# One form of step for a software-pipelined graph layer: transposes one group ahead, second layer in the present group, sums one group behind

## The chip, the cores and the metric

The kernel runs on one core of one Trainium2 chip. The metric is the device time of one execution in microseconds; the time before is the median of three runs. A profile was taken of a further execution of the same program, and all instants below are microseconds from the start of its span.

## What is computed

There are 12,500 nodes with 64 features and 200,000 edges, sorted by their destination. `ssp(v)` is softplus(v) minus ln 2.

```
gates    = (ssp(edge_attr @ We1 + be1) @ We2 + be2) * (1 - sigmoid(5 * (distance - 3.5)))
h        = ssp(concat(x[src], x[dst]) @ Wn1 + bn1) @ Wn2 + bn2
sums     = scatter_add(h * gates, at dst)
new      = x + ssp(sums @ Ws1 + bs1) @ Ws2 + bs2
out      = layernorm(x + new)
```

## The kernel before, in words

**Groups.** The edges are cut into NG = 391 groups of 512: four columns (K = 4) of 128 edges, one edge to a partition. Each step of the main loop (L581 to L655) works on several groups at once, each at another stage.

**The stages of a group g.**
- `gather(g)` (L190): up to four indirect DMAs on POOL bring the 64 source features of each edge into the tile `xg`. They are issued AHEAD = 14 groups ahead; a tile has 18 buffers. 24 of the columns are brought instead row by row by `fetch` (L206): four DMAs on the SP queue and four on the ACT queue in each of the first 384 steps, into `xr`.
- `load(g)` (L225): SP brings the edge features `eT` and, per half of a group, 42 rows of a table (`wns`) that holds the destination's share of the first layer. It is issued five groups ahead.
- `onehot(g)` (L240): DVE writes beside the gathered features a 42-wide one-hot of the destination.
- `transposes(g)` (L247): PE turns the four columns into a PSUM tile `tx`. `xcopy(g)` (L254): ACT copies it to SBUF.
- `layer1_edge(g)` and `layer1_node(g)` (L259, L265): PE writes 768 columns of the first layer to the PSUM tile `z`.
- `exps(g)` and `logs(g)` (L276, L281) on ACT, `softplus(g)` (L284) on DVE.
- `layer2_edge(g)` and `layer2_node(g)` (L290, L300) on PE into `gh`; `hcut(g)` and `message(g)` (L310, L314) on DVE.
- `scatter(g)` (L318): PE sums the messages by their one-hot; `window(g)` (L332): DVE adds the 42-wide result to `sums`.

PSUM tiles `z`, `gh` and `tx` have two buffers each.

**Node blocks.** When enough groups have been summed, a block of up to 512 nodes goes through its own small chain (`node_block`, L339): `hidden` and `layer2` on PE, activations on ACT, small work on DVE, and a store. Its parts are spread over later steps at the distances of BLOCK_STEPS. There are 25 blocks; the last is done after the loop.

**Order of the work.** The order on each engine is the order of the program text (`manual_schedule`); every engine's queue is in order. In the main form of the step (L588 to L618), step i issues on PE: the edge part of the second layer of group i-1, the first layer of group i+1, the sums of group i-3, the transposes of group i+3, and the node part of the second layer of group i-1. The first of these carries added waits for all that the step needs (`needs`, L589 to L592). On ACT the order is `exps(i+1)`, two row DMAs, `logs(i+1)`, two row DMAs, `xcopy(i+3)`. On DVE it is `hcut`, `message`, `window`, the node parts, `softplus(i+1)`, `onehot(i+5)`.

The last ten steps (L619 to L639, CATCH_UP = 10) have another form, in which the lags are taken back one at a time (`lagging`, L562 to L570): transposes, first layer, second layer, sums, in this order.

After the loop (L659 to L695) the last group and the last node block follow.

Of the kernel before, what the change touches and what calls it, by code (L numbers as in the profile page):

```python
# [56 lines left out]
P = 128  # L57
D = 64
HE = 256
GE = 2 * HE  # L60
W = 42
# [4 lines left out]
AHEAD = 14  # L66
LOADS = 5
SPREADS = 5
CATCH_UP = 10
PREPARE = 5  # L70
FREE = 5
BEHIND = 4
# [34 lines left out]
def gnn_resnorm_kernel(ctx: ExitStack, tc: tile.TileContext, a: dict, out: bass.AP, E: int):  # L107
# [18 lines left out]
    def z_tile():  # L126
        return psum.tile([P, 2, NB], F32, name="z")
# [4 lines left out]
    def tx_tile():  # L132
        return psum.tile([P, NB], F32, name="tx")
# [90 lines left out]

    def load(g):  # L225
        eTs[g] = loads.tile([P, HE], F32, name="eT")
        old = ("scatter", g - LOADS - 2 - 4)
        behind(note(("load", g), nc.sync.dma_start(eTs[g], a["eT"][:, g, :])), old)
        if g % 2 == 0:
            _, at = nc.values_load_multi_w_load_instructions(  # L230
                base_i[0:1, 2 * g : 2 * g + 4], engines=[SP], min_val=0, max_val=N - 1,
                skip_runtime_bounds_check_because="they were clamped to these bounds")
            bases[g], bases[g + 1] = at[:2], at[2:]
        for h in range(2):
            behind(note(("load", g), nc.sync.dma_start(wns[D:DW, g % REST, h, :], table[bass.ds(bases[g][h], W), :])),  # L235
                   old)
# [50 lines left out]
        nc.vector.scalar_tensor_tensor(ss[g].rearrange("p i t e -> p (i t e)")[:, part], us[g][:, part], BIG,  # L287
                                       z_of(g)[:, part], OP.min, OP.max)

    def layer2_edge(g, *needs):  # L290
        gh = gh_tile()
        v = gh.rearrange("p (i t h d) -> p i t h d", i=2, t=2, h=2)
        first = nc.tensor.matmul(gh, ones3[:, :P], row3.rearrange("q i k d -> q (i k d)"), start=True, stop=False,  # L293
                                 skip_group_check=True)
        behind(first, *needs)
        for t in range(2):
            nc.tensor.matmul(v[:, 0, t], ss[g][:, 0, t, :], we2, start=False, stop=False, skip_group_check=True)  # L297
        ghs[g] = gh.rearrange("p (i k d) -> p i k d", i=2, k=K)
# [7 lines left out]
    def layer2(g):  # L306
        layer2_edge(g)
        layer2_node(g)
# [118 lines left out]
    with tc.manual_schedule():  # L427
# [128 lines left out]
        with tc.tile_pool(name="finish", bufs=1) as finish:  # L556
            blocks = list(zip(node_blocks(N), block_steps(N, NG)))
            last = NG - 1
            ends = last - CATCH_UP
            second, third, ahead = {}, {}, {}  # L560

            def lagging(i, lag, steps):  # L562

                lag -= sum(i > step for step in steps)
                return [g for g in range(i - lag, i - lag + 1 + (i in steps)) if g >= 0]

            for i in range(-3, NG):
                second[i] = lagging(i, 1, (ends + 3,))
                third[i] = lagging(i, 3, (ends - 2, ends + 5))
                ahead[i] = [i + 3] if i < ends else [i + 2] if i == ends + 1 else [i + 1] if i > ends + 2 else []  # L570
            parts, begun, complete, rest = {}, None, 0, []

            def at(f, g, *more):
                if 0 <= g < NG:
                    f(g, *more)

            for g in range(LOADS - 3):
                load(g)
            for g in range(2):
                onehot(g)  # L580
            for i in range(-3, last - 1):  # L581
                now = parts.pop(i, [])
                early = [part for part in now if part.tensor]
                at(load, i + LOADS)
                fetch(i, nc.sync)
                if i >= 0:
                    at(gather, i + AHEAD, i < BEHIND)
                if i < ends:  # L588
                    needs = [("xcopy", i + 1), ("load", i + 1)]  # L589
                    needs += [(name, g) for g in ahead[i] for name in ("gather", "onehot")]  # L590
                    for g in second[i]:
                        layer2_edge(g, *needs)  # L592
                    if i >= -1:
                        zs[i + 1] = z_tile()
                        layer1_edge(i + 1)
                        for part in early:
                            part.tensor(tx_tile())
                    if i >= -1:
                        layer1_node(i + 1)
                    for n, g in enumerate(third[i]):  # L600
                        scatter(g, zs[i + 1][:, 1, HE + 2 * W * n : HE + 2 * W * (n + 1)])
                    at(exps, i + 1)
                    fetch(i, nc.scalar, 0, ROWS // 2)
                    at(logs, i + 1)
                    fetch(i, nc.scalar, ROWS // 2, ROWS // 2)
                    for g in ahead[i]:
                        transposes(g)
                        xcopy(g)
                    for g in second[i]:
                        layer2_node(g)  # L610
                    for g in second[i]:
                        hcut(g)
                        message(g)
                    for g in third[i]:
                        window(g)
                    for part in early:
                        part.others()
                    at(softplus, i + 1)  # L618
                else:  # L619
                    for g in ahead[i]:  # L620
                        transposes(g)
                        xcopy(g)
                    zs[i + 1] = z_tile()
                    layer1_edge(i + 1)
                    for part in early:
                        part.tensor(zs[i + 1][:, 1, HE:])
                    layer1_node(i + 1)
                    exps(i + 1)
                    logs(i + 1)
                    for g in second[i]:  # L630
                        layer2(g)
                        hcut(g)
                        message(g)
                    softplus(i + 1)
                    for g in third[i]:
                        scatter(g, tx_tile()[:, : 2 * W])
                        window(g)
                    for part in early:
                        part.others()  # L639
                for g in ahead[i]:  # L640
                    at(onehot, g + 2)
                for part in now:
                    if not part.tensor:
                        part.others()
                complete = third[i][-1] + 1 if third[i] else 0
                if blocks and complete >= blocks[0][1] - PREPARE and not begun:
                    begun = node_block(*blocks[0][0], finish)
                    begun.pop(0).others()
                if blocks and complete >= blocks[0][1]:
                    steps = next(steps for steps in BLOCK_STEPS if i + steps[-1] < last - 1)  # L650
                    for n, part in zip(steps, begun):
                        parts.setdefault(i + n, []).append(part)
                    rest = begun[len(steps) :]
                    blocks.pop(0)
                    begun = None  # L655
            assert len(blocks) == 1 and begun and not parts


            begun.pop(2).others()  # L659
            transposes(last)  # L660
            xcopy(last)
            zs[last] = z_tile()
            layer1_edge(last)
            layer1_node(last)
            for some in (edge, node):
                exps(last, some)
                logs(last, some)
            square, variance, root, scale, store = (part.others for part in rest)
            square()
            for g in range(last - 2, last + 1):  # L670
                window_bases(g)
            layer2(last - 1)
            scatter(last - 2, tx_tile()[:, : 2 * W])
            softplus(last, edge)
            hcut(last - 1)
            message(last - 1)
            layer2_edge(last)
            scatter(last - 1, tx_tile()[:, : 2 * W])
            softplus(last, node)
            window(last - 2)  # L680
            variance()
            root()
            layer2_node(last)
            window(last - 1)
            hcut(last)
            message(last)
            scatter(last, tx_tile()[:, : 2 * W])
            window(last)
            hidden, clamp = begun.pop(0)
            hidden(gh_tile())  # L690
            scale()
            clamp()
            store()
            for part in begun:
                node_part(part)  # L695
# [147 lines left out]
```

## Time and profile before

| | |
|---|---|
| median of three runs | 1989.88 us (1989.77 to 1997.46) |
| profiled execution | 1994.42 us, span 1992.6 us |
| granted TensorE clock, mean | 0.977 |
| PE busy | 1843.2 us, 92% of the span |
| DVE, ACT busy | 1082.5 us (54%), 925.0 us (46%) |
| POOL busy | 1463.8 us (73%), 1539 gathers |

A line of the timeline has the start, the duration, the engine, the line of the kernel, the operation, its tiles and shapes and its count; in brackets stands how long the engine was idle before it and what ended that. "issue" means that it waited for nothing that the profile shows. SPq and ACTq are DMA-issuing instructions of these engines. In the table by windows each engine has its busy time and, in brackets, its instructions; then come the granted share of the TensorE clock, the busy share of the DMA engines and the rate.

### The profile page before, as it was taken

What the parts mean: (1) busy time and instruction counts of PE and PEld (TensorE: products, weight loads), DVE (VectorE), ACT (ScalarE), POOL (GpSimd) and SP (SyncE); (2) the same over time, 40 slices, a digit from 0 to 9 for tenths busy, and PEclk for the clock granted to TensorE, in tenths of its full rate; (3) what the DMA queues carried; (4) which work ended last, traced back from release to release, by engine and by line L of the source; (5) the groups of instructions that cost most, each with busy time, mean ns of one, the idle gap of its engine ahead of it and who ended that gap; (6) DMA issues with size and microseconds to landing.
All of it is one profiled execution on the core that took longest, in us unless ns stands there. A gap on an engine that the chain in (4) does not pass through costs nothing.

```text
span 1992.6 us, 46151 instructions
## 1 busy us (share of the span) xinstructions
PE 1843.2 (92%) x11373; PEld 1531.6 (77%) x11373; DVE 1082.5 (54%) x2756; ACT 925.0 (46%) x1318; POOL 1463.8 (73%) x1543
## 2 busy tenths in 40 slices
PE   5899999999998998989999899999999999999996
PEld 4788788888777777777777777777887787787775
DVE  4455455555554554645555555555565555555554
ACT  1355455554444444544444444454454444455442
POOL 6777777777777777777777777777777777777770
PEclk9999899999999999999999999999899999999996
DMA  8422222222222222222232222232232222222230
GB/s 239 131 67 70 63 68 70 69 66 69 67 66 65 65 67 63 66 66 63 68 72 62 68 67 68 63 73 63 68 73 68 68 69 68 69 68 68 71 74 10
DMA packets 173687, 143.41 MB, mean 72 GB/s; under 512 B 49324, under 2 KB 145776, under 8 KB 173415
## 3 DMA queue, kind: packets, MB, share of 16 engines
q1 hardware_dynamic: 119758, 87.95, 15.3%
q0 software_dynamic: 49248, 50.53, 13.2%
q10 hardware_dynamic: 4408, 1.90, 0.4%
q8 instruction: 97, 1.59, 0.3%
q14 instruction: 176, 1.43, 0.2%
HBM read 130.57 MB, written 9.63 MB: 70 GB/s over the span
## 4 chain that ended last, share of the span: by engine, by line
PE 73%; SPq 8%; DMA 7%; issue 5%; DVE 2%; ACT 2%; ACTq 1%; POOL 1%; DVEq 0%; POOLq 0%
PE z L268 15%; PE gh L303 11%; PE gh L297 11%; PE z L262 10%; PE z L320 7%; PE tx L251 6%; PE gh L293 6%; DMA xr<-in_x 6%; PE z L260 3%; SPq L235 3%; SPq L219 2%; SPq L215 2%; PE z L530 2%; ACT u L279 2%; DVE h L312 1%
## 5 line engine op out<-in xcount | busy, mean ns | idle before, releaser
L202 POOL DMA_INDIRECT xg<-in_x,src_i x1539 | 1463.6, 951 | 477.8 <-issue 336.7
L279 ACT ACTIVATE u<-z 128x768 f32<-128x768 f32 x392 | 317.4, 810 | 659.1 <-PE z L320 625.3
L312 DVE TENSOR_TENSOR h<-gh,cut 128x256 f32<-128x256 f32 x391 | 166.1, 425 | 686.1 <-PE gh L303 669.8
L282 ACT ACTIVATE u<-u,one 128x768 f32<-128x768 f32 x392 | 365.9, 933 | 304.4 <-DMA xr<-in_x 294.6
L268 PE MATMUL z<-xT,wns 106*128 106x256 f32 x1564 | 415.9, 389 | 0.0
L303 PE MATMUL gh<-consts,s 128*128 128x64 f32 x3128 | 397.8, 271 | 0.0
L303 PEld LDWEIGHTS gh<-consts,s 128*128 128x128 f32 x3128 | 386.5, 194 | 0.0
L287 DVE SCALAR_TENSOR_TENSOR s<-u,z 128x768 f32<-128x768 f32 x392 | 372.8, 951 | 24.3 <-ACT u L282 7.2
L268 PEld LDWEIGHTS z<-xT,wns 106*128 106x128 f32 x1564 | 302.1, 195 | 44.8 <-ACT xT L256 0.7
L297 PE MATMUL gh<-consts,s 128*128 128x128 f32 x1564 | 280.8, 302 | 0.0
L262 PE MATMUL z<-eT,consts 128*128 128x256 f32 x782 | 277.7, 437 | 0.0
L297 PEld LDWEIGHTS gh<-consts,s 128*128 128x128 f32 x1564 | 205.8, 191 | 92.0 <-issue 91.4
L320 PEld LDWEIGHTS z<-xg,msg 128*128 128x128 f32 x1512 | 234.7, 196 | 21.6
L293 PE MATMUL gh<-row,ones 3*128 3x512 bf16 x391 | 148.9, 381 | 103.1 <-DMA xr<-in_x 47.8
L251 PE MATMUL tx<-consts,xg 128*106 128x128 f32 x1540 | 238.0, 278 | 4.0 <-DVE xg L241 2.7
L256 ACT COPY xT<-tx 106x512 f32<-106x512 f32 x391 | 222.4, 569 | 24.4 <-PE tx L251 15.3
L320 PE MATMUL z<-xg,msg 128*128 128x84 f32 x1512 | 221.6, 269 | 0.0
L337 DVE TENSOR_TENSOR sums<-sums,z 64x42 f32 x756 | 148.5, 196 | 129.9 <-issue 116.7
L251 PEld LDWEIGHTS tx<-consts,xg 128*106 128x106 f32 x1540 | 182.9, 144 | 5.2 <-DVE xg L241 3.0
L316 DVE TENSOR_TENSOR msg<-gh,h 128x256 f32<-128x256 f32 x391 | 165.9, 424 | 13.4
L262 PEld LDWEIGHTS z<-eT,consts 128*128 128x128 f32 x782 | 117.7, 190 | 47.6 <-issue 1.5
L293 PEld LDWEIGHTS <-ones 3*128 3x128 bf16 x391 | 35.5, 91 | 140.2 <-issue 122.1
(101 smaller groups left out, 685.5 us busy)
## 6 DMA issues: line engine op xcount, KB each, us to landing
eT<-in_eT SPq DMA_DIRECT2D x391, 128.0 KB
xg<-in_x,src_i POOLq DMA_INDIRECT x1539
xr<-in_x SPq DMA_DIRECT2D x1536, 0.2 KB
xr<-in_x ACTq DMA_DIRECT2D x1520, 0.2 KB
wns<-table SPq DMA_DIRECT2D x782, 21.0 KB
table<-tb SPq DMA_DIRECT2D x14, 448.0 KB
sums<-in_xT SPq DMA_DIRECT2D x7, 455.0 KB
y<-in_x SPq DMA_DIRECT2D x24, 128.0 KB
```

The costliest lines, as they stand in the source:

```text
L202: note(("gather", g), nc.gpsimd.indirect_dma_start(out=xg[:, k, :D], out_offset=None, in_=x, in_offset=bass.IndirectOffsetOnAxis(ap=src_i[ ...
L251: nc.tensor.transpose(tx[:, k, :], row, ident)
L256: note(("xcopy", g), nc.scalar.copy(xT, xTs[g]))
L262: nc.tensor.matmul(zs[g][:, 0, :HE], we1.rearrange("a h d -> a (h d)"), eTs[g], start=False, stop=True, skip_group_check=True)
L268: nc.tensor.matmul(zn, wns[:, g % REST, h, :], xTs[g][:, h], start=True, stop=True, skip_group_check=True)
L279: nc.scalar.activation(us[g][:, part], z_of(g)[:, part], AF.Exp)
L282: nc.scalar.activation(us[g][:, part], us[g][:, part], AF.Ln, bias=one)
L287: nc.vector.scalar_tensor_tensor(ss[g].rearrange("p i t e -> p (i t e)")[:, part], us[g][:, part], BIG, z_of(g)[:, part], OP.min, OP.max)
L293: first = nc.tensor.matmul(gh, ones3[:, :P], row3.rearrange("q i k d -> q (i k d)"), start=True, stop=False, skip_group_check=True)
L297: nc.tensor.matmul(v[:, 0, t], ss[g][:, 0, t, :], we2, start=False, stop=False, skip_group_check=True)
L303: nc.tensor.matmul(ghs[g][:, 1, 2 * t + h, :], ss[g][:, 1 + h, t, :], wn2, start=False, stop=h == 1 and t == 1, skip_group_check=True)
L320: ins = nc.tensor.matmul(sc, msgs[g][:, 2 * t : 2 * t + 2, :].rearrange("p h f -> p (h f)"), xgs[g][:, 2 * t : 2 * t + 2, D:DW], start=t = ...
```

## The change

The main form and the catch-up form of the step are replaced by one. Step i issues `transposes(i+1)` and `xcopy(i+1)`, the whole first layer of i+1, the activations of i+1, both parts of the second layer of group i, and the sums of group i-1 into a `tx` tile. The lists `second`, `third` and `ahead`, the constant CATCH_UP and the added waits on `layer2_edge` are gone. The loop begins at -1 and not at -3, with four loads ahead of it and not two; `load(g)` names as the older sums that it follows those of group g-9 and not g-11. `complete`, the count of summed groups that starts the node blocks, is i after step i, where the main form had i-2. The four row DMAs of ACT stay between and behind `exps` and `logs`. The code after the loop is the same.

```diff
-        old = ("scatter", g - LOADS - 2 - 4)
+        old = ("scatter", g - LOADS - 2 - 2)
...
-            for g in range(LOADS - 3):
+            for g in range(LOADS - 1):
                 load(g)
...
-            for i in range(-3, last - 1):
+            for i in range(-1, last - 1):
                 now = parts.pop(i, [])
                 early = [part for part in now if part.tensor]
                 at(load, i + LOADS)
                 fetch(i, nc.sync)
                 if i >= 0:
                     at(gather, i + AHEAD, i < BEHIND)
-                if i < ends:
...
-                else:
...
+                transposes(i + 1)
+                xcopy(i + 1)
+                zs[i + 1] = z_tile()
+                layer1_edge(i + 1)
+                for part in early:
+                    part.tensor(zs[i + 1][:, 1, HE:])
+                layer1_node(i + 1)
+                exps(i + 1)
+                fetch(i, nc.scalar, 0, ROWS // 2)
+                logs(i + 1)
+                fetch(i, nc.scalar, ROWS // 2, ROWS // 2)
+                if i >= 0:
+                    layer2(i)
+                    hcut(i)
+                    message(i)
+                softplus(i + 1)
+                if i >= 1:
+                    scatter(i - 1, tx_tile()[:, : 2 * W])
+                    window(i - 1)
+                    complete = i
+                for part in early:
+                    part.others()
+                at(onehot, i + 3)
```

More of the change, by code (lines that the diff above doesn't have):

```diff
@@ L68 @@
 SPREADS = 5
-CATCH_UP = 10
 PREPARE = 5
@@ L288, in softplus, with layer2_edge @@
                                        z_of(g)[:, part], OP.min, OP.max)
-    def layer2_edge(g, *needs):
+    def layer2_edge(g):
         gh = gh_tile()
         v = gh.rearrange("p (i t h d) -> p i t h d", i=2, t=2, h=2)
-        first = nc.tensor.matmul(gh, ones3[:, :P], row3.rearrange("q i k d -> q (i k d)"), start=True, stop=False,
-                                 skip_group_check=True)
-        behind(first, *needs)
+        nc.tensor.matmul(gh, ones3[:, :P], row3.rearrange("q i k d -> q (i k d)"), start=True, stop=False,
+                         skip_group_check=True)
         for t in range(2):
@@ L558, in gnn_resnorm_kernel @@
             last = NG - 1
[L559 to L570, printed above, removed]
             parts, begun, complete, rest = {}, None, 0, []
@@ L587, in gnn_resnorm_kernel @@
                     at(gather, i + AHEAD, i < BEHIND)
-                if i < ends:
[L589 to L618, printed above, removed]
-                else:
[L620 to L639, printed above, removed]
@@ L640, in gnn_resnorm_kernel @@
-                for g in ahead[i]:
-                    at(onehot, g + 2)
+                transposes(i + 1)
[9 more added lines that the diff above has]
+                fetch(i, nc.scalar, ROWS // 2, ROWS // 2)
@@ L644, in gnn_resnorm_kernel @@
                         part.others()
-                complete = third[i][-1] + 1 if third[i] else 0
                 if blocks and complete >= blocks[0][1] - PREPARE and not begun:
```

## The prediction, made before the changed kernel was run

> **What bounds the kernel now.** I read first the page's table of 40 slices and its costliest groups:
>
> ```profile
> POOL 6777777777777777777777777777777777777770
> ...
> L202 POOL DMA_INDIRECT xg<-in_x,src_i x1539 | 1463.6, 951 | 477.8 <-issue 336.7
> ```
>
> POOL shows sevens from beginning to end, which looks like room. It is not. Its timeline shows why:
>
> ```profile
> 1937.18 0.94 POOL L202 DMA_INDIRECT xg<-in_x,src_i  x1 [0.30 <-DMA xg<-in_x,src_i]
> 1938.43 0.94 POOL L202 DMA_INDIRECT xg<-in_x,src_i  x1 [0.30 <-PE tx L251]
> 1939.68 0.95 POOL L202 DMA_INDIRECT xg<-in_x,src_i  x1 [0.30 <-issue]
> 1940.93 0.94 POOL L202 DMA_INDIRECT xg<-in_x,src_i  x1 [0.30 <-issue]
> ```
>
> Every gather takes 0.94 and is followed by 0.30 in which nothing is waited for, whatever releaser is named: 1.25 each. 1539 x 1.25 = 1924 us; the first starts at 3.2, the last ends at 1941.9. POOL never waits longer than 0.3 save at the start (by the list of its waits, 2.8 us for the indices and 6.6 us for two memsets). A group of four gathers costs POOL 5.0 us, on average 4.93.
>
> Next I set PE beside POOL, by counting the gathers group by group (four, less those that the code leaves out) against the transposes. From the end of a group's last gather to its first transpose passed 65.7 us for group 0, 30.2 for group 50, 7.8 for group 90, then 4.7 to 7 for nearly all up to group 382, and 21.7 for group 390. So PE, which starts late (first transpose 73.7), runs freely for some 95 steps, catches up, and then follows POOL. Near the end it falls behind again. These are the windows of a free step, of a step in the last ten (the other form), and of such a step at half clock:
>
> ```profile
> 1006.03:1010.38 4.35, 4.35 (x30) 3.66 (x29) 2.51 (x7) 2.54 (x5) 3.13 (x5) 1.00 0.36 90
> 1936.03:1940.53 4.50, 4.50 (x29) 3.36 (x28) 2.38 (x7) 2.63 (x5) 3.59 (x4) 1.00 0.23 55
> 1959.60:1967.81 8.21, 8.21 (x29) 6.19 (x28) 3.18 (x8) 2.33 (x4) 0.00 (x0) 0.50 0.01 2
> ```
>
> The first column is the length from one `exps` to the next: 4.35, 4.50 and 8.21. The third number from the right is the granted clock. So PE at 92% busy is not the bound between steps 95 and 380: it needs 4.35 of POOL's 4.93. The bound is POOL up to 1941.9, and then a PE tail of 50.7 us.
>
> **The change part by part.**
>
> *The new step is already in the trace.* The catch-up form has the new order: transposes, first layer, second layer, sums. Its plain step takes 4.50 (twice: 1936.03 to 1940.53 and 1947.73 to 1952.24), 0.15 over 4.35. What is lost stands between PE's rows: the first layer waits for `xcopy`, and the second layer starts 0.3 late. What those steps lack is the four row DMAs on ACT. ACT's rows of a free step and of that form:
>
> ```profile
> 1006.03 0.81 ACT L279 ACTIVATE u<-z 128x768 f32<-128x768 f32 x1 [1.02 <-PE z L320]
> 1006.73 0.84 ACTq L219 DMA_DIRECT2D xr<-in_x  x2
> 1007.62 0.94 ACT L282 ACTIVATE u<-u,one 128x768 f32<-128x768 f32 x1 [0.78 <-DMA xr<-in_x]
> 1007.77 0.61 ACTq L219 DMA_DIRECT2D xr<-in_x  x2
> 1008.47 0.57 ACT L256 COPY xT<-tx 106x512 f32<-106x512 f32 x1
> ```
>
> ```profile
> 1936.03 0.81 ACT L279 ACTIVATE u<-z 128x768 f32<-128x768 f32 x1 [1.22 <-PE z L268]
> ...
> 1938.72 0.59 ACT L256 COPY xT<-tx 106x512 f32<-106x512 f32 x1 [0.61 <-PE tx L251]
> 1940.53 0.81 ACT L279 ACTIVATE u<-z 128x768 f32<-128x768 f32 x1 [1.22 <-PE z L268]
> ```
>
> With row DMAs, ACT is ready for the copy 2.44 after `exps` starts (1008.47 - 1006.03): the first pair opens a gap of 0.78, the second pair lies under `logs`. In the new form the copy waits for PE's transposes until 2.69 after (1938.72 - 1936.03). So ACT has 0.25 to spare, and the plain step stays 4.50. Behind the copy in ACT's queue stands `exps`, which needs that copy through PE anyway: 1.81 from copy to `exps`, so ACT's circle is 2.44 + 1.81 = 4.25.
>
> *Node parts.* On PE, `hidden` takes 0.86 and `layer2` 0.88 of a step (their four matmuls and one bias); put between the edge and the node part of the first layer, each covers the 0.24 wait for the copy: 0.62 + 0.64. On ACT the two activations of a block (0.93), the square (0.42) and the root (0.51) use up the 0.25 and delay the copy by 0.68, 0.17 and 0.26. Together 2.4 us a block; 24 x 2.4 = 57 us, 0.15 a step. Mean step 4.65.
>
> *Does PE still keep up?* 73.7 + 390 x 4.65 = 1887 for the last transposes, against 1941.9 + 1.8 by POOL. (1.8 is the landing: in the steps bound by POOL the distance was seldom under 4.8, of which PE's work from the waiting instruction at L293 to the transposes is 2.98, 1007.20 to 1010.18.) PE catches up near step 150, not 95. That costs nothing; the mean step may grow to (1943.7 - 73.7) / 390 = 4.79 before it does.
>
> *The gathered waits.* They go, and with them some semaphore instructions ahead of L293. The wait for the gathers now sits on the transposes; behind it on PE stand the whole first layer, the second layer of i and the sums of i-1, and for them ACT and DVE. While POOL is the bound this costs nothing. Lower bound 0, upper bound through the clock (first rival).
>
> *Moves that I cost at nothing.* The loads, SP's row DMAs and POOL's gathers keep their order. SP's circle was about 4.4 a step and gets more room. Rows for `xr` must be there at step 35, not 33; the 3.15 us stall that PE had at 221 goes, under slack. On DVE `softplus` now passes `window` (0.41) and the clamps (0.95), which wait for no one. The sums move from `z` to `tx`; a `tx` buffer is free 4.0 after `exps`, its next use comes 6.1 after. The memsets that precede gathers 14 to 17 come a little later on DVE: 0 to 2 us of POOL, I take 1.
>
> *The end* is where time goes. In the last ten steps the old kernel does the delayed stages as well, and block 22's scaling (DVE) stands ahead of block 23's `ssp`. PE waits 2.02 for that and drops to half clock:
>
> ```profile
> 1957.96 0.74 PE L387 MATMUL z<-consts,l_s 128*128 128x128 f32 x4 [2.02 <-DVE l_s L379]
> ...
> 1963.50:1992.50 29.00, 17.32 (x60) 12.92 (x59) 11.13 (x35) 5.34 (x13) 0.00 (x0) 0.50 0.04 12
> ```
>
> (The first line is of the timeline, the second of the windows: the stretch from the last transposes to the end, at clock 0.50.) In the new one, `complete` is ahead by two, so block 22 is scaled in step 385 and block 23's `ssp` comes in step 386. The transposes follow POOL: group 384 at 1915.4 + 1.8 = 1917.2, 385 at 1922.2, 386 at 1927.4; then PE: 387 at +5.1 (`hidden`) = 1932.5, 388 at 1937.0, 389 at +5.1 (`layer2`) = 1942.1, 390 at 1946.6. Before: 1963.5. From there the old kernel needs 29.1 us. At full clock I get 7.6 less: transposes and first layer 2.4 and not 4.2; about 5.3 off the 13.1 from there to the end of the last `hidden` (1967.77 to 1980.85), by halving the second layers, sums and `hidden` where ACT and DVE don't set the pace; 0.45 off its second layer. Bounds 21.5 to 29.1; the chain has gaps that may drop the clock, so I take the middle, 25.3. For PE being late after a drop of the clock shortly before I add 2.5 (before, such steps cost 1.5 to 3 over 5.0).
>
> Sum: 1946.6 + 25.3 + 2.5 + 1 = 1975.4 against 1992.6, -17. The profiled execution took 1994.4, 4.5 over the median of 1989.9; taken off the median, 1972 to 1973. I say 1972. With full clock and no lateness: 1964. With half clock and 7 us of lateness: 1981.
>
> **A rule of the Trainium skill against the row.** A wait of 1.21 was enough to halve the clock for 13 us:
>
> ```profile
> 1398.72 0.37 PE L293 MATMUL gh<-row,ones 3*128 3x512 bf16 x1 [1.21 <-DMA xr<-in_x]
> ...
> 1399.70:1413.00 13.30, 13.30 (x48) 11.03 (x47) 4.22 (x11) 3.58 (x5) 9.96 (x11) 0.50 0.23 52
> ```
>
> (Timeline, then windows.) The Trainium skill, "TensorE: Matmul & The Clock Gate", Part 1, has the clock halve after a whole idle window of about 3.4 us; by that none of the new waits would count, and this row contradicts it. The same page, "A second HAM failure mode: psum-queue depth-cycling", says that frequent short idling between groups of matmuls makes the clock swing; that speaks against the change. If it halved the clock in every other step, the mean step would be an estimated 6.5 and the time over 2500 us, which no stretch of this trace resembles.
>
> **The rivals.**
>
> *First, slower: the clock.* The old step bound by POOL idles mostly in one place (L293, some 0.6). The new one idles 0.4 at the transposes, then 0.1, 0.2 and 0.3 within the next 2.3 us: up to 1.0 in 3.4 us. A step at half clock costs 8.21 - 4.50 = 3.7 more. Outside the end, half clock covered 58 us in the old run (3%), in eleven places, ten of them while PE followed POOL. For: 0.7 to 1.2 of idling sufficed several times. Against: the catch-up steps kept full clock through these same gaps, and after a drop PE is late, so has no wait until it has caught up. It decides above a mean of 4.79, that is 4% of steps at half clock without a wait for POOL. At 8%: 4.65 + 0.30 = 4.95, last transposes at 2004, end 2033, on the median's scale about 2030.
>
> *Second, slower: ACT becomes the bound.* Copy, `exps` and `logs` are now one circle with PE, and the row DMAs lie in it. The gap of 0.78 was 1.1 at most. If DMA waits add 0.75 to a step, the circle is 5.0: last transposes 2024, end about 2049, so 2045. It decides from 0.5 more per step; nothing in the old rows comes near.
>
> *Third, no change:* the end keeps half clock and the blocks crowd it again: 1981 to 1995, say 1985.
>
> **How the numbers follow.** Forecast 0.55, first rival 0.21, second 0.11, third 0.13. About 0.5% (10 us) is what a measurement here can tell from no change. Faster 0.55, same 0.13, slower 0.32. The forecast's own range is 1963 to 1981; the range reaches to 2040, which takes in most of the first rival.
>
> **What the new profile would show.** Right: gathers still 1.25 apart with the last near 1942; `exps` 4.50 apart up to about step 150; transposes about 2 us behind their last gather after that; group 390 transposed near 1947 to 1952. Wrong: gathers that wait for PE's sums, more than 100 us at half clock before 1940, or copies that start at once when ACT is free.

## The result

| | before | after |
|---|---|---|
| median | 1990.4 us (1989.8 to 1997.5, 4 runs) | 2270.6 us (2233.3 to 2305.9, 4 runs) |
| ratio after / before | | 1.129, 95% interval 1.115 to 1.144 |
| profiled execution, span | 1994.4, 1992.6 us | 2305.9, 2304.1 us |
| at half clock, in all | 93 us, 12 stretches | 572 us, 16 stretches |
| last gather ends | 1941.9 | 2183.6 |
| group 390 transposed | 1963.5 | 2280.2 |
| from there to the end | 29.1 | 23.9 |

The change makes the kernel 13% slower; I had said 1% faster. All of the loss lies before the last transposes. In this profile the end itself is shorter; in a second profile of the same kernel (f0 below) it takes 29.3, all at half clock. (Ratios here and below compare the fast runs alone, which are here those of 2233 and 2266 us, at mean clocks of 0.915 and 0.900; the profiled execution is the longest of the four, at 0.876.)

The page of after, in 40 slices, its chain, and three groups:

```profile
POOL 6677777767677777775766555765777555477500
PEclk9999889979899999997998667977999766599877
...
PE 60%; SPq 14%; DMA 11%; issue 6%; ACT 5%; DVE 2%; ACTq 2%; DVEq 0%
...
L201 POOL DMA_INDIRECT xg<-in_x,src_i x1539 | 1462.1, 950 | 721.0 <-issue 361.0
...
L267 PE MATMUL z<-xT,wns 106*128 106x256 f32 x1564 | 491.4, 442 | 105.6 <-ACT xT L255 103.3
...
L255 ACT COPY xT<-tx 106x512 f32<-106x512 f32 x391 | 227.8, 583 | 262.0 <-PE tx L250 191.0
```

POOL's row of sevens is broken, and the gathers' idle time grew from 477.8 to 721.0. The clock has holes all along the run. DMA and SP's queue hold a quarter of the chain. POOL's timeline, some 40 us earlier than the stretch shown of before:

```profile
1899.25 0.94 POOL L201 DMA_INDIRECT xg<-in_x,src_i  x1 [0.30 <-issue]
1900.49 0.94 POOL L201 DMA_INDIRECT xg<-in_x,src_i  x1 [0.30 <-issue]
1904.96 0.94 POOL L201 DMA_INDIRECT xg<-in_x,src_i  x1 [3.52 <-PE tx L250]
```

POOL now waits for PE (for a free `xg`). By the count used for the prediction, PE never catches up with the gathers: 54 to 117 us lie between a group's last gather and its first transpose during the whole run. So the bound is PE's step. Taken over steps 20 to 377, it is 5.05 where the clock is full (286 steps) and 8.13 where it is halved (72 steps). 113 of the full-clock steps take 4.50, as predicted. Some of the others hold node parts; most are long because the copy starts late. The list of waits names it:

```profile
ACT u L281 <- DMA xr<-in_x: 366.2, 383, 2.8
...
PEld z L267 <- ACT xT L255: 195.8, 281, 2.8
ACT xT L255 <- PE tx L250: 191.0, 204, 3.2
...
PE z L267 <- ACT xT L255: 103.3, 128, 2.4
```

(Engine, line, what it waited for, then us in all, times, longest.) Before, the first line was 294.6, 368 times, at most 1.1. Now PE waits at the node part of the first layer (L267) for the copy, and before ACT's `logs` there are gaps of up to 2.8.

### The profile page after: what moved, and what is told of

Its sections match the earlier page's. It is cut to its first block, busy times and chain, and to the rows that moved or that the text cites. A ratio compares the mean times of both kernels' runs of the same rounds, so it can differ in the third digit from the quotient of the medians.

```text
span 2304.1 us, 45402 instructions
## 1 busy us (share of the span) xinstructions
PE 2139.8 (93%) x11373; PEld 1589.0 (69%) x11373; DVE 1058.6 (46%) x2756; ACT 958.8 (42%) x1318; POOL 1462.3 (63%) x1543
## 4 chain that ended last, share of the span: by engine, by line
PE 60%; SPq 14%; DMA 11%; issue 6%; ACT 5%; DVE 2%; ACTq 2%; DVEq 0%
PE z L267 14%; PE gh L301 12%; PE gh L295 9%; DMA xr<-in_x 7%; PE tx L318 6%; PE tx L250 5%; PE z L261 5%; SPq L218 4%; SPq L234 4%; PE gh L292 4%; ACT xT L255 3%; SPq L214 3%; SPq L229 2%; DMA wns<-table 2%; ACTq L218 2%
## 5 line engine op out<-in xcount | busy, mean ns | idle before, releaser
L201 POOL DMA_INDIRECT xg<-in_x,src_i x1539 | 1462.1, 950 | 721.0 <-issue 361.0
L310 DVE TENSOR_TENSOR h<-gh,cut 128x256 f32<-128x256 f32 x391 | 166.1, 425 | 1100.5 <-PE gh L301 1096.3
L267 PE MATMUL z<-xT,wns 106*128 106x256 f32 x1564 | 491.4, 442 | 105.6 <-ACT xT L255 103.3
L267 PEld LDWEIGHTS z<-xT,wns 106*128 106x128 f32 x1564 | 313.3, 216 | 240.3 <-ACT xT L255 195.8
L301 PE MATMUL gh<-consts,s 128*128 128x64 f32 x3128 | 448.1, 293 | 0.0
L301 PEld LDWEIGHTS gh<-consts,s 128*128 128x128 f32 x3128 | 439.9, 217 | 0.0
L295 PE MATMUL gh<-consts,s 128*128 128x128 f32 x1564 | 311.4, 327 | 0.0
L261 PE MATMUL z<-eT,consts 128*128 128x256 f32 x782 | 310.9, 483 | 0.4 <-DMA eT<-in_eT 0.4
L295 PEld LDWEIGHTS gh<-consts,s 128*128 128x128 f32 x1564 | 229.9, 211 | 101.8 <-issue 89.8
L318 PE MATMUL tx<-xg,msg 128*128 128x84 f32 x1564 | 277.2, 305 | 1.1 <-DVE msg L314 1.1
L250 PE MATMUL tx<-consts,xg 128*106 128x128 f32 x1540 | 264.5, 300 | 2.7 <-DVE xg L240 2.7
L318 PEld LDWEIGHTS tx<-xg,msg 128*128 128x128 f32 x1564 | 236.8, 217 | 1.2 <-issue 1.2
L250 PEld LDWEIGHTS tx<-consts,xg 128*106 128x106 f32 x1540 | 204.9, 157 | 3.3 <-DVE xg L240 3.0
L335 DVE TENSOR_TENSOR sums<-sums,tx 64x42 f32 x782 | 150.7, 193 | 7.8 <-PE tx L318 0.8
```

Source lines behind the costliest of these rows:

```text
L201: note(("gather", g), nc.gpsimd.indirect_dma_start(out=xg[:, k, :D], out_offset=None, in_=x, in_offset=bass.IndirectOffsetOnAxis(ap=src_i[ ...
L250: nc.tensor.transpose(tx[:, k, :], row, ident)
L261: nc.tensor.matmul(zs[g][:, 0, :HE], we1.rearrange("a h d -> a (h d)"), eTs[g], start=False, stop=True, skip_group_check=True)
L267: nc.tensor.matmul(zn, wns[:, g % REST, h, :], xTs[g][:, h], start=True, stop=True, skip_group_check=True)
L301: nc.tensor.matmul(ghs[g][:, 1, 2 * t + h, :], ss[g][:, 1 + h, t, :], wn2, start=False, stop=h == 1 and t == 1, skip_group_check=True)
L318: ins = nc.tensor.matmul(sc, msgs[g][:, 2 * t : 2 * t + 2, :].rearrange("p h f -> p (h f)"), xgs[g][:, 2 * t : 2 * t + 2, D:DW], start=t = ...
```

## Two theories

**Theory 1:** the row DMAs delay the copy. They stand in ACT's queue in front of it, and the copy, once made two steps ahead of its use, is now in the middle of PE's step. **Theory 2:** the order itself, with several short waits of PE in each step, costs the clock, whatever the row DMAs do.

The trace gave theory 1 a mechanism. Each DMA record names the semaphore on which it reports, and the queues of SP and ACT share eight of them. In the compiled order each of these DMAs waits until the earlier one on its semaphore has landed. In after, SP issued a row DMA at 1003.88; it landed at 1005.28; ACT's row DMA on the same semaphore was issued at 1005.30, and the copy behind it began at 1005.57. This is the rule and not one case: in after's full-clock steps from 36 to 377, ACT's second pair takes over 0.9 in 83, and in 82 of them its last DMA is issued 0.02 after the landing of SP's earlier DMA on the same semaphore. In f0, the same kernel once more, it is 99 of 100, and nearly all of these DMAs of SP are rows.

## The experiments

There were 18 runs. In two of the six batches the kernel before took 1988 to 2003 us, as in the case; in the other four it took 2552 to 2607. I tell the two first, since only they bear on the sizes. Edits are against the changed kernel.

### The changed kernel again, without row DMAs, and two groups ahead

`f0_after_again` is the changed kernel once more.

> The changed kernel once more, as the mark for the runs beside it. Where the kernel before takes 1990 both theories expect 2233 to 2306 (ratio 1.12 to 1.16) and 300 to 570 us at half clock; where the chip is as in the first experiments (before at 2570 to 2600), both expect a ratio of 1.05 to 1.12.

**Measured:** 2219.9 us (2198 to 2246), before 1994.6, ratio 1.103 (1.098 to 1.107); 446 us at half clock. A little less loss than in the first measurement, the same picture. It is the mark for what follows.

`f1_no_rows`: all 24 columns are gathered by POOL.

```diff
-    half_of = {nc.sync: 0, nc.scalar: len(by_rows) // 2}
+    by_rows = []
+    half_of = {nc.sync: 0, nc.scalar: 0}
...
-                fetch(i, nc.sync)
...
-                fetch(i, nc.scalar, 0, ROWS // 2)
...
-                fetch(i, nc.scalar, ROWS // 2, ROWS // 2)
```

> The changed order without any row DMA: all 24 columns go to POOL's gathers (24 x 1.25 = 30 us more on POOL). Theory 1 (the row DMAs that SP and ACT issue delay the copy, and PE's waits for the copy cost the steps and the clock): the copy starts 2.7 after exps throughout, plain steps are 4.5, under 100 us at half clock before 1900, and the time is that of POOL: 1985 to 2030 where before takes 1990, ratio 1.00 to 1.02. Theory 2 (the order itself, with several short waits of PE in each step, costs the clock): half clock stays over 300 us and the time within 3% of the changed kernel beside it.

**Measured:** 2014.8, ratio 1.012 (1.008 to 1.016), clock 0.988. Plain steps 4.50, 19 us at half clock before the last transposes.

`f2_no_act_rows`: only ACT's 12 columns go to POOL. (Not shown: `half_of` and the bound in `fetch` now count SP's columns alone.)

```diff
-    return [(g, k) for k in (K - 1, K - 2) for g in range(P // ROWS + 4, NG - 2, P // ROWS)]
+    return [(g, k) for k in (K - 1,) for g in range(P // ROWS + 4, NG - 2, P // ROWS)]
...
-                fetch(i, nc.scalar, 0, ROWS // 2)
...
-                fetch(i, nc.scalar, ROWS // 2, ROWS // 2)
```

> The changed order with ACT's half of the row DMAs done by POOL (15 us more on POOL); SP keeps its four a step. Theory 1: the copy no longer stands behind row DMAs in ACT's queue, so most of the loss goes: 1980 to 2060 where before takes 1990, and less than half of the changed kernel's loss wherever it is measured. Theory 2: within 3% of the changed kernel beside it.

**Measured:** 2002.4, ratio 1.005 (1.003 to 1.007). From step 20 to 120 the mean step is 4.54, and PE catches up with POOL near step 140.

`f3_two_ahead`: the row DMAs stay; transposes and copy are one group further ahead. (Not shown: one more `onehot` ahead of the loop, and the last transposes and copy no longer behind it.)

```diff
-                transposes(i + 1)
-                xcopy(i + 1)
+                if i < 0:
+                    transposes(i + 1)
+                    xcopy(i + 1)
+                at(transposes, i + 2)
+                at(xcopy, i + 2)
...
-                at(onehot, i + 3)
+                at(onehot, i + 4)
```

> The changed order with the transposes and the copy of group i+2 in place of i+1, all else as changed; the row DMAs stay. Theory 1: a copy that is late by up to 2.4 is still done a step before PE needs it, so PE's waits for the copy fall under 50 us in all (from 299), and the time is 1970 to 2030 where before takes 1990. Theory 2: PE has the same number of matmuls and gaps elsewhere, half clock stays over 300 us and the time within 3% of the changed kernel beside it.

**Measured:** 1987.1 (1979.6 to 2008.2), ratio 0.999 (0.996 to 1.003). PE's waits at L267 for the copy are gone from the list of waits (110.2 us in f0); the plain step is 4.40.

The clock rows of the four, in this order:

```profile
PEclk9978999999899999997996689977987998899965
```

```profile
PEclk9999999999999999999999999999999999999995
```

```profile
PEclk9999999999999999999989999999999999999995
```

```profile
PEclk9999999999699999997999997999899999999998
```

**What follows.** Theory 2 falls. f1 and f2 have the new order with all its short waits of PE and keep the clock; f3 has all row DMAs and loses nothing, since a copy that is late is not needed yet.

### Whose row DMAs: SP's rows away, ACT's kept

`i0_no_sp_rows` (not shown: `half_of` and the bound in `fetch`, as in f2):

```diff
-    return [(g, k) for k in (K - 1, K - 2) for g in range(P // ROWS + 4, NG - 2, P // ROWS)]
+    return [(g, k) for k in (K - 2,) for g in range(P // ROWS + 4, NG - 2, P // ROWS)]
...
-                fetch(i, nc.sync)
```

> The changed order without SP's row DMAs, ACT's two pairs a step kept, once more, for a chip on which the kernel before takes 1990. On the slower chip it brought ACT's second pair back from over 0.9 us in 34% of the steps to 1%. Theory 1a (SP's rows on shared semaphores hold ACT's back): 1995 to 2040 there. Theory 1b (ACT's own four issues are enough): 2130 to 2230. On a chip where before takes over 2500 the ratio is 1.06 again.

**Measured:** 2003.0, ratio 1.003 (1.001 to 1.006), 23 us at half clock, although ACT still issues its two pairs in front of the copy. So ACT's own four issues were as harmless as the prediction had them; SP's four are what makes ACT's wait. The same place in f0 and in i0, by the timeline (lines of ACT and its queue, SP's queue, and PE's L267):

```profile
1024.32 0.81 ACT L278 ACTIVATE u<-z 128x768 f32<-128x768 f32 x1 [1.22 <-PE z L267]
...
1024.81 1.50 SPq L218 DMA_DIRECT2D xr<-in_x  x4
...
1025.21 0.84 ACTq L218 DMA_DIRECT2D xr<-in_x  x2
...
1026.10 0.94 ACT L281 ACTIVATE u<-u,one 128x768 f32<-128x768 f32 x1 [0.98 <-DMA xr<-in_x]
...
1026.61 1.09 ACTq L218 DMA_DIRECT2D xr<-in_x  x2
...
1027.74 0.58 ACT L255 COPY xT<-tx 106x512 f32<-106x512 f32 x1 [0.70 <-DMA xr<-in_x]
...
1028.38 1.13 PE L267 MATMUL z<-xT,wns 106*128 106x256 f32 x4 [0.56 <-ACT xT L255]
...
1028.93 1.50 SPq L218 DMA_DIRECT2D xr<-in_x  x4
...
1029.55 0.81 ACT L278 ACTIVATE u<-z 128x768 f32<-128x768 f32 x1 [1.22 <-PE z L267]
...
1031.36 0.61 ACTq L218 DMA_DIRECT2D xr<-in_x  x2
...
1032.25 0.58 ACT L255 COPY xT<-tx 106x512 f32<-106x512 f32 x1
...
1034.05 0.81 ACT L278 ACTIVATE u<-z 128x768 f32<-128x768 f32 x1 [1.22 <-PE z L267]
```

```profile
699.55 0.81 ACT L278 ACTIVATE u<-z 128x768 f32<-128x768 f32 x1 [2.00 <-PE z L267]
...
700.24 0.85 ACTq L218 DMA_DIRECT2D xr<-in_x  x2
...
701.13 0.94 ACT L281 ACTIVATE u<-u,one 128x768 f32<-128x768 f32 x1 [0.78 <-DMA xr<-in_x]
...
701.58 0.61 ACTq L218 DMA_DIRECT2D xr<-in_x  x2
...
702.24 0.59 ACT L255 COPY xT<-tx 106x512 f32<-106x512 f32 x1 [0.17 <-PE tx L250]
```

In f0's first step SP's four rows are issued from 0.49 after `exps` on, beside ACT's pairs. ACT's second pair takes 1.09 instead of 0.61, the copy begins 3.42 after `exps` instead of 2.70, and the step is 5.23. In the next one SP's rows come 0.62 before `exps`; the pair takes 0.61 and the step 4.50. Sorted by how many of SP's rows are issued within 2.2 us after `exps`, f0's full-clock steps from 36 on are:

| SP rows in that time | steps | copy after `exps` | step |
|---|---|---|---|
| 0 to 2 | 117 | 2.73 | 4.66 |
| 3 | 63 | 3.00 | 4.91 |
| 4 | 117 | 3.59 | 5.47 |

Of ACT's 1536 row DMAs, 374 were issued within 1.6 us of SP's DMA on the same semaphore in f0, none in i0, and 7 (of 1520) in the kernel before. (There ACT fetches in 380 steps, not 384: the last ten have no row DMAs on ACT, so 16 rows for group 388 are never fetched, which the changed kernel does.) In f3 there are 207, and PE waits for no copy behind them.

The Trainium skill, "DMA: Bandwidth & Descriptors", Anatomy of one DMA, a section on POOL's DMAs, says that DMA engines do not wait on semaphores and that any such wait happens on the issuing sequencer before dispatch. That agrees with what the lines above show for ACT: it is idle for 0.70 before the copy, behind a queue entry that does no work of ACT's.

### How much of it is the clock

`i1_fill`: two matmuls more per step, between edge and node part; their result is overwritten.

```diff
+                if not early:
+                    for _ in range(2):
+                        nc.tensor.matmul(zs[i + 1][:, 1, HE:], we1.rearrange("a h d -> a (h d)"), eTs[i + 1],
+                                         start=True, stop=True, skip_group_check=True)
                 layer1_node(i + 1)
```

> The changed kernel with two matmuls more per step between edge and node part, once more, for a chip on which the kernel before takes 1990. If half clock is a cost of its own beside the late copy, under 150 us of half clock are left (from 446) and the time is 2080 to 2160. If half clock only marks steps that are late anyway, 2200 to 2300. On a chip where before takes over 2500 the ratio is 1.01 to 1.02 again.

**Measured:** 2186.6, ratio 1.097 (1.094 to 1.100): between the two. Half clock is all but gone (13 us), though late copies remain (27% of the second pairs take over 0.9). But I had taken the two matmuls for hidden, and they are not: in a plain step the wait is 0.24, and they make 1.03, so a plain step takes 5.27 (4.50 + 0.77) and the mean one 5.33: with 73.4 for the start and 22.4 for the end, 390 of them are 2175 of the span's 2178. So half clock is a cost of its own and can be had back, at a price nearly as high. In f0 the steps from 20 to 377 are 5.03 at full clock and 7.99 where half clock touches them (49 of 358): about 390 x 49/358 x 2.96 = 158 us of the run. The two runs bear this out: i1's steps are 0.30 longer than f0's at full clock, 117 us in 390 steps, and yet its span is 64 shorter.

In after one drop looks like this (timeline, then windows):

```profile
1878.83 3.48 ACTq L218 DMA_DIRECT2D xr<-in_x  x2
...
1882.36 0.59 ACT L255 COPY xT<-tx 106x512 f32<-106x512 f32 x1 [2.74 <-DMA y<-in_x]
...
1882.99 1.13 PE L267 MATMUL z<-xT,wns 106*128 106x256 f32 x4 [2.41 <-ACT xT L255]
```

```profile
1884.10:1942.10 58.00, 58.00 (x201) 43.85 (x201) 18.18 (x47) 17.84 (x26) 25.03 (x28) 0.50 0.16 37
```

ACT has been idle for 2.74 when the copy starts: its second pair took 3.48, since the last DMA of it shares its semaphore with SP's load of `y` for a node block, which landed at 1882.07. PE waits 2.41, and for 58 us the clock is halved while PE is busy without a gap by the profile. Both profiles of the changed kernel together give, for PE's waits at L267 at full clock:

| wait | times | a drop follows |
|---|---|---|
| under 0.8 | 181 | 0 |
| 0.8 to 1.2 | 66 | 8 |
| 1.2 to 1.6 | 25 | 12 |
| over 1.6 | 12 | 10 |

30 of the 36 drops follow such a wait. The Trainium skill, "TensorE: Matmul & The Clock Gate", Part 1, has the clock halve after an idle window of about 3.4 us and come back after a busy one as long. Neither holds here: waits of 0.8 to 2.4 are followed by half clock, and stretches last up to 68 us with PE busy. Nor is 0.8 us a threshold: in the kernel before, three drops follow waits at L293 of 0.45, 0.75 and 0.78. What holds the clock down so long stays open.

### The runs in which the kernel before took 2552 to 2607

Twelve runs fell there. Their mechanism differs, as this timeline of `g0_no_sp_rows` shows (PE, then DVE):

```profile
2084.40 1.00 PE L301 MATMUL gh<-consts,s 128*128 128x64 f32 x8
...
2087.30 0.42 DVE L310 TENSOR_TENSOR h<-gh,cut 128x256 f32<-128x256 f32 x1 [3.17 <-PE z L261]
```

DVE starts 1.90 after the matmuls that it waits for have ended by the profile. In the profiles where before takes 1990 (before, after, f0 to f3, i0, i1) this distance, from the last matmul into `gh` to L310, is 0.04 in nearly every step; in these twelve it is over 1.9 in a tenth of the steps, and in e6 about 1.3 or more in every second one. So DVE hears late of PE's work, or PE's work ends later than the profile models. An order with more handovers in a row would suffer more from that; this was not tried by itself. The jobs' chip numbers don't part the two conditions. What causes them is open.

| run | edit | before | this | ratio (95%) | clock |
|---|---|---|---|---|---|
| e1_no_act_rows | as f2 | 2567 | 2679 | 1.049 (1.041 to 1.056) | 0.79 |
| e2_no_sp_rows | as i0 | 2567 | 2742 | 1.067 (1.062 to 1.072) | 0.74 |
| e3_rows_after_copy | ACT's four rows between copy and `exps` | 2567 | 2731 | 1.066 (1.062 to 1.070) | 0.76 |
| e5_two_ahead | as f3 | 2567 | 2708 | 1.055 (1.049 to 1.062) | 0.76 |
| e4_before_no_needs | kernel before without its gathered waits | 2597 | 2582 | 0.995 (0.993 to 0.997) | 0.83 |
| e6_fill | as i1 | 2597 | 2649 | 1.022 (1.018 to 1.025) | 0.92 |
| e7_old | the load waits as in the kernel before | 2597 | 2896 | 1.114 (1.109 to 1.120) | 0.72 |
| g0_no_sp_rows | as i0 | 2562 | 2725 | 1.062 (1.056 to 1.068) | 0.74 |
| g1_pair_after_copy | ACT's second pair between copy and `exps` | 2562 | 2743 | 1.061 (1.051 to 1.071) | 0.74 |
| g2_fill | as i1 | 2562 | 2598 | 1.012 (1.007 to 1.017) | 0.92 |
| g3_before_no_needs | as e4 | 2562 | 2550 | 0.995 (0.993 to 0.998) | 0.84 |
| h1_pair_after_copy | as g1 | 2561 | 2777 | 1.071 (1.062 to 1.081) | 0.72 |

The edits not shown yet: e4 and g3 (against the kernel before), e7, and g1 and h1; e3 moves both pairs to the place to which g1 moves the second.

```diff
-                        layer2_edge(g, *needs)
+                        layer2_edge(g)
```

```diff
-        old = ("scatter", g - LOADS - 2 - 2)
+        old = ("scatter", g - LOADS - 2 - 4)
```

```diff
                 xcopy(i + 1)
+                fetch(i - 1, nc.scalar, ROWS // 2, ROWS // 2)
...
-                fetch(i, nc.scalar, ROWS // 2, ROWS // 2)
```

What was expected of them, in the order of the table:

> The changed kernel with the twelve columns that ACT fetched row by row gathered by POOL (12 x 1.25 = 15 us more on POOL, last gather near 1957). Theory 1 (ACT's row DMAs wait for other transfers to land, so the copy of the transposes comes late, PE waits for it, and a long wait halves the clock): copies start 2.7 us after exps, mean step at full clock 4.6 to 4.8 (5.05 in the changed kernel), under 100 us at half clock (572), time 1975 to 2010. Theory 2 (the new order with its small gaps loses the clock by itself): over 300 us at half clock, time over 2150.

> The changed kernel with the twelve columns that SP fetched row by row gathered by POOL; ACT's row DMAs stay. If ACT's row DMAs are late because they wait for SP's transfers to land (theory 1, by way of semaphores that both queues share), the waits go and the time is 1975 to 2020. If issuing them on ACT is itself the cost, copies stay as late as in the changed kernel and the time is over 2150. Theory 2: over 2150.

> The changed kernel with ACT's four row DMAs put between the copy and exps, where ACT waits 1.2 us for PE anyway. Theory 1: the copy is late by them no longer; exps may be late by about 1 us, but PE does not wait for exps in the same step. Mean step at full clock 4.6 to 4.9, under 200 us at half clock, time 1980 to 2060. Theory 2: over 2150.

> The changed kernel with transposes and copy two groups ahead, all else alike, row DMAs in their place. Theory 1: a late copy is then a step early, PE does not wait for it; mean step at full clock 4.4 to 4.7 until POOL binds, under 120 us at half clock, time 1970 to 2010. Theory 2 (order and small gaps between matmuls): over 2150.

> The kernel before with the added gathered waits on the second layer left out, lags kept. Theory 3 (the gathered waits keep the clock up): over 200 us at half clock (93 before), time over 2050. Theory 1 (lags are what counts): within 1% of before, 1975 to 2010.

> The changed kernel with two more matmuls (the edge layer's shape, into columns of z that nobody reads) between the edge and the node part of the first layer in each step without node matmuls: some 0.85 us of work where PE waits for the copy. The waits on ACT stay. If waits of PE halve the clock: under 200 us at half clock, step 5.1 to 5.4, time 2080 to 2180, faster than the changed kernel in spite of more work. If the new order loses the clock by itself: 500 us or more at half clock, time 2400 or more.

> The changed kernel with load(g) behind the sums of group g-11 again and not g-9: SP is released at another point of the step. Theory 1 with the shared semaphores: ACT's waits for SP's transfers shift, the time changes by over 2% (2200 or less if SP's transfers land earlier). If the release of SP plays no part: same as the changed kernel, 2230 to 2310.

> The changed order with SP's half of the row DMAs done by POOL (15 us more on POOL); ACT keeps its two pairs a step, the second between logs and copy. Theory 1a (an issue on ACT waits until SP's row DMA on the same completion semaphore has landed): with SP's rows gone, ACT's pairs take their usual 0.6 to 0.8, the copy starts at most 2.75 after exps in most steps, and the time is 1995 to 2040 where before takes 1990. Theory 1b (ACT's own four issues in front of the copy are enough): most of the loss stays, 2130 to 2230.

> The changed order with ACT's second pair of row DMAs put between copy and exps (1.23 us free there in a plain step), not between logs and copy; nothing else moves, POOL has its 1539 gathers. If the failed step of the prediction is only that this pair lies under logs, the copy starts 2.7 after exps again, plain steps are 4.5 and the time is 1965 to 1990 where before takes 1990. If a pair there waits as long as it did in front of the copy, exps is late instead, and the time stays over 2080.

> The changed kernel with two matmuls more per step on PE, whose result the node part overwrites, between the edge part and the node part, where PE waits for a late copy; the row DMAs and the late copies stay. It parts the two costs of a late copy. If the half clock after such waits is a cost of its own, under 150 us of half clock are left (from 446 to 572) and the time falls to 2080 to 2160 although PE has more to do. If half clock only marks steps that are late anyway, the time is 2200 to 2300.

> The kernel before with one part of the change alone: the gathered waits ahead of the second layer are gone, the lags and the order stay. Both theories expect no loss, 1978 to 1992 where before takes 1990 (ratio 0.994 to 1.001), since copy and rows stay three groups ahead. If the gathered waits kept the clock up, half clock grows over 150 us and the time goes over 2010.

> The changed order with ACT's second pair of row DMAs between copy and exps, once more, for a chip on which the kernel before takes 1990. If the failed step of the prediction is only that this pair lies under logs, the copy starts 2.7 after exps again, plain steps are 4.5 and the time is 1965 to 1990. If a pair there waits as long as it did in front of the copy, exps is late instead, and the time stays over 2080. Where before takes over 2500, the ratio is 1.06 again and nothing is told apart.

**What follows.** The times told for 1990 can't be compared, and the changed kernel itself was not run here, so what an edit gains on it is not known; e7, the nearest to it, is 11% slow. e1, e2, e3 and e5, for which theory 1 had promised times near the kernel before, stay 5 to 7% slow, so another cost is left here. Three things hold all the same. The gathered waits have no part in the loss: the kernel before without them is 0.5% faster, twice (e4, g3), though under this condition alone. Taking SP's rows away frees ACT's queue here too: ACT's second pair takes over 0.9 in 1% of g0's full-clock steps, against 34% in f0, and in 96% of them in e7, whose earlier loads move SP's rows but don't part them from ACT's. And keeping PE busy (e6, g2) brings the clock to 0.92, and the time nearer to the kernel before than any other edit of the new order here. Whether moving ACT's second pair behind the copy would mend the change where before takes 1990 (g1, h1) stays untried.

## Why the prediction was wrong

**Right.** The plain step of 4.50 is in all runs of the new order (after, f0, f1, f2, i0). Node parts cost about what was priced: in f1 their two steps take 5.95 and 5.28, 2.2 a block over 4.50, against 2.4. Without the collision the mean of steps 20 to 120 is 4.54 (f1, f2) to 4.58 (i0); these steps hold two of the 24 blocks, so they say nothing against the 4.65 for the whole run. PE then catches up near step 140 in f1 and f2, against 150 (in i0, where ACT keeps its rows, near 180). That was in part luck: by the mean of 4.65 PE gains 0.28 a step on POOL's 4.93 and needs some 230 steps; 150 goes with the plain step, and it came near because few blocks fall so early. The gathered waits, DVE's order and the `tx` buffers cost nothing that shows in these steps. One small slip: by its own terms the forecast with full clock and no lateness is 1966, not 1964.

**The step that failed** is "the second pair lies under `logs`. ... So ACT has 0.25 to spare", and behind it, among the moves costed at nothing, "SP's row DMAs ... keep their order. SP's circle was about 4.4 a step and gets more room". ACT's 0.25 is right when ACT's DMAs find their semaphores free: the copy starts 2.70 after `exps` then, and 3.59 where SP's rows fall beside ACT's pairs. I looked at each queue's length and not at what the two share. The sign was in the trace of before, in SP's own waits, which I read as SP's matter:

```profile
SPq L228 <- DMA xr<-in_x: 91.8, 124, 3.9
SPq L219 <- DMA xr<-in_x: 79.0, 106, 4.2
```

The same view of after:

```profile
SPq L227 <- PE tx L250: 642.0, 354, 6.2
```

Before, SP was the one that waited for rows to land, 171 us in two lines, and there it was harmless. Now SP is held by PE: the load waits for the sums of group g-9 (the view names L250, which follows them on PE), and SP's four rows follow it, often beside ACT's pairs. Where a row DMA of ACT follows a row DMA of SP on its semaphore (steps 36 to 377), SP's belonged to the step before in 597 of 626 cases in the kernel before, and had mostly landed long ago; in f0 all 710 belong to two steps later, since SP's queue is that far ahead, and are often just issued. Whether the room put SP ahead, or the order in which the compiled program hands out the semaphores, was not tried. The wait has changed sides, from a queue with room to the one in front of the copy.

**The sum, mis-sized.** With the prediction's 4.65 the last transposes would be at 73.7 + 390 x 4.65 = 1887 if POOL allowed it. Late copies, priced at nothing, add 390 x (5.05 - 4.65) = 156, half clock 390 x 72/358 x (8.13 - 5.05) = 242: 2285, against 2280.2 measured. POOL's bound of 1943.7 hides the first 57 us of it.

**The rivals.** The second rival had the mechanism (row DMAs in ACT's circle) and took 0.75 a step for it; measured were 0.40 on the mean full-clock step (5.05 against 4.65), and 0.81 in f0 between steps where all four of SP's rows fall beside ACT's (5.47) and those where at most two do (4.66). It "decides from 0.5 more per step", but "nothing in the old rows comes near" was wrong, and it brought the first rival with it: a late copy is a wait of PE, and waits over 1.2 were followed by half clock in 22 of 37 cases. Against that rival I had held that "after a drop PE is late, so has no wait until it has caught up". That is so for waits for POOL; the copy is late however late PE is. The two costs were priced apart, each alone, and the range ended where the larger one would.

**The end.** 17 us were to come from there. In f2 and i0, where the collision is gone, the last transposes come at 1967 and 1973, not 1946.6. The reason is mostly POOL: it has 12 gathers more there, 12 x 1.25 = 15 us, and its last one ends at 1956.2 and 1961.8, not 1941.9. In f3, which has the 1539 gathers of the forecast, the last transposes come at 1950.0, near the 1946.6, and the end takes 27.8 against 25.3 predicted. That profile's span is 1977.8, near the forecast's 1975.4, though of another order, and it is of the shortest of ten runs; their median is 1987.1 and the longest took 2008, and where those lose it is not on record. How long the end takes goes with the clock: 29.0 to 29.5 where all of it is at half clock (before, f0, f1, f2), and 21.9 to 27.8 where 11 to 17 us of it are (after, f3, i0, i1). No version tried is clearly faster than the kernel before where that takes 1990.

## What to carry to other kernels

Before putting a stage of an engine into another's step, look at what shares the queue with it, and on which semaphores the DMAs there report: a DMA in front of a copy can wait for another queue's transfer to land. A queue that runs ahead can turn such a wait round. A wait that moves from a queue with slack to one in the bound's circle costs nearly all of itself, the more so when the stage behind it was steps ahead and is now needed at once. And where waits of about 1 us on TensorE are followed by half clock, as here, price a delay and the clock together.

## What the runs showed of the hardware

- In f0 a row DMA of ACT that needs the semaphore of a row DMA of SP follows it by 1.17 us at the least; of those under 1.6 the median is 1.38. That is what one short transfer costs a queue that shares semaphores.
- In the two profiles of the changed kernel, waits at L267 under 0.8 us were never followed by half clock (181 cases), those over 1.6 nearly always (10 of 12); in the kernel before, waits at L293 of 0.45, 0.75 and 0.78 were. In after and f0, 34 of the 36 halved stretches, of 3.4 to 68 us, had TensorE busy throughout by the profile.
- The same program takes 1990 or 2560 to 2600 us. In the slower condition VectorE starts its work on `gh` 1.9 us or more after TensorE's matmuls end by the profile in a tenth of the steps, not 0.04.
